# Layer 0 of a graph network: scores from x through one folded matrix, and h by rows only

## The chip, the cores and the metric

The kernel runs on one core of a Trainium2 chip. The metric is the device time of one execution in microseconds. A core has five engines that run side by side, each with its own queue of instructions: TensorE (PE in the profile; its weight loads are listed apart as PEld), VectorE (DVE), ScalarE (ACT), GpSimd (POOL) and SyncE (SP), which here issues loads. Within an engine the instructions go in the order in which they were built. Waits between engines go through semaphores.

## The reference

Four layers work on 16 batches of 1024 nodes with 128 features, `x`, and a 0/1 adjacency matrix `adj` of 1024 by 1024 per batch. Each layer adds its result to `x` and normalizes the rows. Only layer 0 is touched here:

```
h = x @ W_w.T + W_b
e = einsum('bjl,bkl->bjk', h @ A, h);  e = e + swapaxes(e, 1, 2)
att = where(adj > 0, e, -9e15);  att = softmax(att, axis=1) * adj
h_prime = relu(einsum('bij,bjk->bik', att, h))
coeff = sigmoid(concat([x, h_prime]) @ gate_w.T + gate_b)
x = layernorm(x + coeff * x + (1 - coeff) * h_prime)
```

Layer 1 thins out the adjacency row by row and then runs three steps of neighbour averaging; layer 2 is a second attention, and layer 3 a convolution on the graph.

Since e is summed with its transpose, e[j,k] = h_j (A + A') h_k. With h = W x + b this is x_j · (M x_k + v), where M = W'(A + A')W and v = W'(A + A')b, plus terms that hold no j. The softmax runs over j, so a term without j leaves it as it is.

## The kernel before

The work is written with pools of buffers and a framework that orders the instructions of each engine ahead of the run, by its own estimate of when each can start, and sets the semaphores. So the order on an engine isn't that of the source. The kernel has a fast path for the expected inputs, with checks collected in a flag, and a general kernel behind it that runs only where the flag is set.

In layer 0 three generators are interleaved by `in_turn`: `before` (batch b+1), `attention` (batch b) and `after` (batch b-1).

`before` goes through the eight blocks of 128 rows of the adjacency. For each, SP loads 512 KB into a ring of three buffers `an`; ScalarE turns it into 8-bit form (`carry` in the profile, L922) and sums the degree; VectorE checks the part right of the diagonal (L927); TensorE turns the finished blocks with narrow products (`pt`, L934), and VectorE compares them with the row block (`chk`, L935). Between these blocks the operands of the attention are made, all in float32: after block 1 the transpose `xT` of the rows `xn`; after block 3 `hT` = W0 xT + b0 and a part of the gate; after block 5 `G` = -As0 hT, with As0 = A + A'; after block 7 `hn`, which is `hT` turned back to rows. All of these, the `pt` products and the gates go through one pool of PSUM, `ps_h`, with two buffers of 512 columns.

`attention` takes eight blocks of 128 nodes k. ScalarE makes the mask (`msk`, L969); TensorE makes the negated scores of a block in two halves, with a block of `hT` as the stationary operand and `G` as the moving one (`pmm`, L724, in a pool `ps_w` of two buffers of 1024 columns); VectorE adds the mask and takes the minimum (`em`, `mx`, L972); ScalarE takes the exponential and its sum (L974); VectorE takes the reciprocal and scales a block of `hn` by it (`hs`, L976 and L978); TensorE accumulates `hs` times the exponentials into `acc` (L981). The two products of one block share the same `em` ring of two buffers.

`after` takes relu of `acc` as `hpT` (L987), makes the gate, turns `hpT`, mixes it with `xn` on VectorE (L998 to L1001) and normalizes the rows (`normed`): statistics on VectorE, a power on GpSimd (L745), a combined factor on VectorE (`ln_nb`, L799), and eight passes on ScalarE (L801).

A helper line stands for many operations in the profile: L724 is `wide_matmul`, L759 the turns, L766 the products over 512 columns, L775 the gates. `products` and `turned` yield a half of a result at a time, and the reading instruction follows in the source.

At the start the raw weights lie in a pool `l0_raw` that is closed before the pool `l0_work` is opened; the first buffer of `xn` lies where the raw weights lay. All loads of the layer go through SP's queue.

Of the kernel before, what the change touches and what calls it, by code (L numbers as in the profile page):

```python
# [9 lines left out]
F32 = mybir.dt.float32  # L10
# [5 lines left out]
FP8 = mybir.dt.float8e4  # L16
# [623 lines left out]
def fast_kernel(ctx: ExitStack, tc: tile.TileContext, t: dict, out: bass.AP, flag: bass.AP):  # L640
# [65 lines left out]
    def transposed(pool, psum, src, name, tag="tr"):  # L706
        v = pool.tile([P, P], F32, name=name)
        p = psum.tile([P, P], F32, name="wtr", tag=tag)
        nc.tensor.transpose(p, src, identf)
        nc.vector.tensor_copy(v, p)  # L710
        return v
# [178 lines left out]
    with ExitStack() as ph:  # L890

        early = ph.enter_context(tc.tile_pool(name="l0_early", bufs=1, reuse_waits="tile"))
        wts = ph.enter_context(tc.tile_pool(name="l0_w", bufs=1, reuse_waits="tile"))
        ps_w = ph.enter_context(tc.tile_pool(name="l0_pw", bufs=2, space=PSUM, reuse_waits="tile"))
        ps_a = ph.enter_context(tc.tile_pool(name="l0_pa", bufs=1, space=PSUM, reuse_waits="tile"))
        ps_h = ph.enter_context(tc.tile_pool(name="l0_ph", bufs=2, space=PSUM, reuse_waits="tile"))

        with tc.tile_pool(name="l0_raw", bufs=1) as raw:
            W0T = transposed(wts, ps_h, matrix(raw, t["L0_gnn_W_w"], "l0W"), "l0WT", "h")
            As0 = symmetric(wts, ps_h, matrix(raw, t["L0_gnn_A"], "l0A"), "l0As", "h")  # L900
        work = ph.enter_context(tc.tile_pool(name="l0_work", bufs=1, reuse_waits="tile"))
        small = ph.enter_context(tc.tile_pool(name="l0_small", bufs=2, reuse_waits="tile"))
        b0 = column(wts, t["L0_gnn_W_b"], "l0b")
        gw = wts.tile([P, 2, 32], F32, name="l0gw")
        nc.vector.memset(gw, 0.0)
        with nc.allow_non_contiguous_dma(reason="a vector of 256"):
            nc.sync.dma_start(gw[:, :, 0], t["L0_gnn_gate_w"].rearrange("o (h d) -> d (o h)", d=P))
        gb = row_bcast(wts, t["L0_gnn_gate_b"], 1, "l0gb")
        gbh = wts.tile([P, 1], F32, name="l0gbh")
        nc.vector.tensor_scalar(gbh, gb, 0.5, None, op0=OP.mult)  # L910
        nbig = wts.tile([P, 1], F32, name="l0nbig")
        nc.vector.memset(nbig, BIG)

        def before(s, b):

            s.xn = work.tile([P, NT, P], F32, name="xn", bufs=3)
            nc.sync.dma_start(s.xn, nat(t["x"][b]))
            for it in range(NT):
                c = b * NT + it
                an = early.tile([P, N], F32, name="an", bufs=3)  # L920
                nc.sync.dma_start(an, t["adj"][b][it * P:(it + 1) * P, :])
                nc.scalar.activation(Y[b][:, it, :], an, AF.Copy, accum_out=deg[:, c:c + 1], saturate=False)  # L922

                chk = early.tile([P, N], FP8, name="chk")
                done = (it + 1) * P
                if done < N:
                    nc.vector.scalar_tensor_tensor(chk[:, done:], an[:, done:], 0.0, an[:, done:], op0=OP.is_gt,  # L927
                                                   op1=OP.not_equal, accum_out=other[:, 3 * c:3 * c + 1], saturate=False)
                for h in range(it // 4 + 1):
                    js = range(4 * h, min(4 * h + 4, it + 1))  # L930
                    k = slice(js[0] * P, (js[-1] + 1) * P)
                    pt = ps_h.tile([P, 512], F32, name="pt", tag="h")
                    for i, jt in enumerate(js):
                        nc.tensor.matmul(pt[:, i * P:(i + 1) * P], Y[b][:, jt, it * P:done], identb, start=True, stop=True)  # L934
                    nc.vector.scalar_tensor_tensor(chk[:, k], pt[:, :k.stop - k.start], 0.0, an[:, k], op0=OP.is_gt,  # L935
                                                   op1=OP.not_equal, accum_out=other[:, 3 * c + h + 1:3 * c + h + 2],
                                                   saturate=False)
                if it == 1:
                    xT = early.tile([P, N], F32, name="xT")
                    for p, c, _ in turned(ps_h, s.xn):  # L940
                        nc.scalar.copy(xT[:, c], p)
                elif it == 3:
                    s.hT = work.tile([P, N], F32, name="hT", bufs=2)
                    for p, c in products(ps_h, (W0T, xT)):
                        nc.scalar.activation(s.hT[:, c], p, AF.Identity, bias=b0)
                    pz = gates(ps_h, early.tile([P, N], FP8, name="chk").bitcast(F32), (gw[:, 0, :], xT))
                    s.gx = small.tile([P, NT], F32, name="gx")
                    nc.vector.tensor_copy(s.gx.rearrange("p (q t) -> p q t", t=2), pz[:, :, :, 0])
                elif it == 5:
                    s.G = work.tile([P, N], F32, name="G", bufs=2)  # L950
                    for p, c in products(ps_h, (As0, s.hT)):
                        nc.scalar.activation(s.G[:, c], p, AF.Copy, scale=-1.0)
                elif it == 7:
                    s.hn = work.tile([P, N], F32, name="hn")
                    for p, c, _ in turned(ps_h, s.hT):
                        nc.vector.tensor_copy(s.hn[:, c], p)
                yield
            nc.gpsimd.dma_start(adj8_d[b], Y[b].bitcast(F32))

        def attention(s, b):  # L960


            s.acc = ps_a.tile([P, N], F32, name="acc")
            for jt in range(NT):
                js = slice(jt * P, (jt + 1) * P)
                c = b * NT + jt
                mn = mx0[:, c:c + 1]
                msk = work.tile([P, N], BF16, name="msk", bufs=2)
                nc.scalar.activation(msk, Y[b][:, jt, :], AF.Identity, scale=-BIG, bias=nbig)  # L969
                e = wide_matmul(ps_w, s.hT[:, js], s.G)  # L970
                em = work.tile([P, N], F32, name="em", bufs=2)
                nc.vector.tensor_tensor_reduce(em, e, msk, 1.0, 3.0e38, op0=OP.add, op1=OP.min, accum_out=mn)  # L972
                sm = small.tile([P, 1], F32, name="sm")
                nc.scalar.activation(em, em, AF.Exp, scale=-1.0, bias=mn, accum_out=sm)  # L974
                rs = small.tile([P, 1], F32, name="rs")
                nc.vector.reciprocal(rs, sm)  # L976
                hs = small.tile([P, P], F32, name="hs")
                nc.vector.tensor_scalar(hs, s.hn[:, js], rs, None, op0=OP.mult)  # L978
                for h in range(H2):
                    c = slice(h * 512, (h + 1) * 512)  # L980
                    nc.tensor.matmul(s.acc[:, c], hs, em[:, c], start=(jt == 0), stop=(jt == NT - 1))  # L981
                yield

        def after(s, b):

            hpT = work.tile([P, N], F32, name="hpT")
            nc.scalar.activation(hpT, s.acc, AF.Relu)  # L987
            pz = gates(ps_h, work.tile([P, NT, P], F32, name="r").rearrange("p t d -> p (t d)")[:, :N // 4], (gw[:, 1, :], hpT))
            co = small.tile([P, NT], F32, name="co")
            nc.vector.tensor_add(co.rearrange("p (q t) -> p q t", t=2), pz[:, :, :, 0],  # L990
                                 s.gx.rearrange("p (q t) -> p q t", t=2))
            nc.scalar.activation(co, co, AF.Tanh, scale=0.5, bias=gbh)
            cx = small.tile([P, NT], F32, name="cx")
            nc.vector.tensor_scalar(cx, co, 0.5, 1.5, op0=OP.mult, op1=OP.add)
            nc.vector.tensor_scalar(co, co, -0.5, 0.5, op0=OP.mult, op1=OP.add)
            yield
            r = work.tile([P, NT, P], F32, name="r")
            nc.vector.tensor_mul(s.xn, s.xn, per_row(cx))  # L998
            for p, c, k in turned(ps_h, hpT):
                nc.vector.tensor_mul(r[:, k, :], tiles3(p), half_rows(co[:, k]))  # L1000
            nc.vector.tensor_add(s.xn, s.xn, r)  # L1001
            yield
            normed(small, s.xn)
            nc.gpsimd.dma_start(nat(x1_d[b]), s.xn)
            yield

        in_turn(before, attention, after)
# [746 lines left out]
```

## Time and profile before

| What | Value |
|---|---|
| Median of 3 runs | 2961.86 us (2958.01 to 2962.2) |
| The profiled execution | 2964.0 us |
| Its span, first to last instruction | 2962.2 us |
| TensorE busy, share of the span | 2725.4 us, 92% |
| TensorE weight loads | 1695.2 us, 57% |
| VectorE busy | 2196.2 us, 74% |
| ScalarE busy | 2024.2 us, 68% |
| GpSimd busy | 325.8 us, 11% |
| First accumulation of layer 0 starts (L981) | 36.5 us |
| First and last relu of `acc` (L987) | 74.2 and 674.3 us |

Busy times overlap between engines. The ends of matmul records are modelled, so that two following records of TensorE overlap in the profile; the distance between their starts is what one costs in a row. A float32 product shows as two records. An "idle before" of an engine is put down to what released it last; where it says "issue", the profile shows nothing that it waited for. The median of the three runs and the profiled execution are different executions.

### The profile page before, as it was taken

Reading aid. Unit: us, or ns where it says so; the run is one execution under the profiler, and the core shown is the slowest. Engines: PE = TensorE matmul, PEld = TensorE weight load, DVE = VectorE, ACT = ScalarE, POOL = GpSimd, SP = SyncE. Lnnn points to the kernel's source line nnn. Section 1 sums busy time; section 2 is a strip of 40 time slices with the busy share of each in tenths; the row PEclk is TensorE's granted clock in tenths of the full one; section 3 lists DMA queues with packets and bytes.
Section 4 is the critical chain, followed back from the end, with each engine's and each line's share of the span. In section 5 each row is a group of like instructions: output and inputs, shape, how many; then the busy total and the mean of one; then the engine's idle time right before and its main releaser. Section 6 shows DMA issues by size and latency. Waiting matters only on the chain.

```text
span 2962.2 us, 42088 instructions
## 1 busy us (share of the span) xinstructions
PE 2725.4 (92%) x14771; PEld 1695.2 (57%) x14834; DVE 2196.2 (74%) x6087; ACT 2024.2 (68%) x3476; POOL 325.8 (11%) x295
## 2 busy tenths in 40 slices
PE   7999999996999889999899988999999999999996
PEld 3444444443666657877788873555555555555554
DVE  5777777777999976776688785777777777776765
ACT  6788888874788786666555435666666667676753
POOL 0000000030000001111122230001000101000000
PEclk9999999997999999999999997999999999999998
DMA  5444444420000052233467681111111111111000
GB/s 187 135 157 151 163 163 157 151 91 16 2 2 2 2 195 82 100 107 136 162 212 266 228 327 50 47 62 64 61 68 69 60 58 57 57 57 57 22 15 23
DMA packets 124125, 297.91 MB, mean 101 GB/s; under 512 B 12672, under 2 KB 65664, under 8 KB 116736
## 3 DMA queue, kind: packets, MB, share of 16 engines
q1 hardware_dynamic: 103440, 211.65, 21.6%
q0 software_dynamic: 20464, 83.47, 7.1%
q8 instruction: 119, 1.95, 0.3%
q14 instruction: 102, 0.84, 0.1%
HBM read 211.04 MB, written 84.02 MB: 100 GB/s over the span
## 4 chain that ended last, share of the span: by engine, by line
PE 36%; issue 19%; DVE 17%; POOL 4%; ACT 4%; DMA 2%; SPq 0%; POOLq 0%; DVEq 0%; ACTq 0%
PE ph L1550 8%; PE acc L1306 7%; PE ph L766 5%; PE acc L1626 4%; PE ph L1410 3%; PE pmm L724 3%; POOL ln_rstd L745 2%; PE ph L759 2%; DVE ln_st L794 2%; PE ph L1536 2%; DVE em L1612 2%; ACT xn L801 2%; POOL rn L745 1%; DVE A L1679 1%; PE acc L981 1%
## 5 line engine op out<-in xcount | busy, mean ns | idle before, releaser
L724 PE MATMUL pmm<-G,hT 128*128 128x512 f32 x1024 | 512.8, 614 | 10.7 <-DVE mx L1612 6.7
L801 ACT ACTIVATE xn<-xn,ln_nb,ln_rstd 128x128 f32<-128x128 f32 x512 | 207.4, 481 | 112.9 <-DVE ln_nb L799 112.8
L724 PEld LDWEIGHTS pmm<-G,hT 128*128 128x128 f32 x1024 | 175.0, 193 | 166.7 <-issue 118.3
L745 POOL TENSOR_TENSOR ln_rstd<-ln_rstd,mhalf 128x8 f32<-128x8 f32 (+1 forms) x68 | 115.9, 1704 | 1323.9 <-DVE nmx L1614 606.7
L1306 PE MATMUL acc<-a,lo 128*128 128x512 f32 x768 | 243.5, 401 | 15.5 <-DVE lo L1273 15.5
L1626 PE MATMUL acc<-em,hs 128*128 128x512 f32 x512 | 251.8, 611 | 3.5 <-DVE hs L1623 1.9
L981 PE MATMUL acc<-em,hs 128*128 128x512 f32 x512 | 245.7, 601 | 6.5 <-DVE hs L978 5.6
L1306 PE MATMUL acc<-a,hi 128*128 128x512 f32 x768 | 244.1, 402 | 3.7 <-ACT hi L1272 3.5
L1145 ACT ACTIVATE q<-s,negc 128x512 f16<-128x512 f32 x256 | 170.6, 697 | 59.2 <-DVE negc L1124 22.3
L1143 PE MATMUL s<-step,carry 128*128 128x384 bf16 (+3 forms) x1034 | 199.4, 304 | 7.9 <-DVE carry L1113 3.2
L1157 ACT ACTIVATE carry<-pc,negone 128x512 fp8e4<-128x512 f32 x256 | 166.8, 699 | 38.3 <-PE pc L1156 28.9
L972 DVE CUSTOM_DVE_ANT_0 em<-pmm,msk 128x1024 f32<-128x1024 f32 x128 | 155.9, 1218 | 40.6 <-PE acc L981 20.3
L1306 PEld LDWEIGHTS acc<-a,lo 128*128 128x128 f32 x768 | 144.4, 190 | 54.8 <-DVE lo L1273 21.1
L1612 DVE CUSTOM_DVE_ANT_0 em<-pmm,msk 128x1024 f32<-128x1024 f32 x128 | 155.6, 1216 | 25.9 <-PE acc L1626 21.3
L922 ACT ACTIVATE carry<-an 128x1024 fp8e4<-128x1024 f32 x128 | 134.4, 1050 | 50.7 <-DMA an<-in_adj 50.5
L1306 PEld LDWEIGHTS acc<-a,hi 128*128 128x128 f32 x768 | 143.0, 190 | 37.1 <-ACT hi L1272 4.0
L1607 ACT ACTIVATE msk<-A,nbig 128x1024 bf16<-128x1024 fp8e4 x128 | 145.9, 1140 | 26.6 <-DVE mx L1612 23.4
L974 ACT ACTIVATE em<-em,mx 128x1024 f32<-128x1024 f32 x128 | 146.0, 1141 | 25.4 <-DVE mx L972 22.7
L981 PEld LDWEIGHTS acc<-em,hs 128*128 128x128 f32 x512 | 90.9, 189 | 123.9 <-issue 87.2
L1410 PE MATMUL ph<-Wx,hT 128*128 128x128 f32 x768 | 153.4, 282 | 3.0 <-ACT nT L1435 1.4
L1410 PE MATMUL ph<-Wr,ag 128*128 128x128 f32 x768 | 151.1, 279 | 1.4 <-DMA ag<-ag_d 1.2
L1666 ACT CAST A<-A 128x1024 fp32r<-128x1024 fp8e4 x64 | 64.2, 1040 | 124.8 <-PE ph L1550 124.6
(294 smaller groups left out, 6181.9 us busy)
## 6 DMA issues: line engine op xcount, KB each, us to landing
an<-in_adj SPq DMA_DIRECT2D x128, 512.0 KB, 3.5
adj_d<-carry POOLq DMA_DIRECT2D x16, 1024.0 KB, 4.2
A<-dil_d SPq DMA_DIRECT2D x16, 1024.0 KB, 7.1
rdeg<-rdeg_d SPq DMA_DIRECT2D x32, 512.0 KB, 4.2
ag_d<-ag POOLq DMA_DIRECT2D x32, 512.0 KB, 5.3
ag<-ag_d SPq DMA_DIRECT2D x32, 512.0 KB, 6.3
A<-adj_d SPq DMA_DIRECT2D x16, 1024.0 KB, 4.7
xn<-in_x SPq DMA_DIRECT2D x16, 512.0 KB, 4.2
```

What stands on the lines that cost most here:

```text
L724: nc.tensor.matmul(p[:, h * 512:(h + 1) * 512], lhsT, rhs[:, h * 512:(h + 1) * 512], start=True, stop=True)
L745: nc.gpsimd.tensor_tensor(r, r, mhalf[:, :n], op=OP.pow)
L801: nc.scalar.activation(r[:, k.start + i, :], r[:, k.start + i, :], AF.Identity, scale=rstd[:, i:i + 1], bias=nb[:, i:i + 1])
L981: nc.tensor.matmul(s.acc[:, c], hs, em[:, c], start=(jt == 0), stop=(jt == NT - 1))
L1143: nc.tensor.matmul(s[:, lo or 0:], y, twos if lo is None else step[:, :512 - lo], start=(j == 0), stop=(j == len(terms) - 1))
L1145: nc.scalar.activation(q[:, h * 512:(h + 1) * 512], s, AF.Abs, bias=st.negc[:, i:i + 1])
L1157: nc.scalar.activation(Y[b][:, hb, ks], pc, AF.Relu, bias=negone, saturate=False)
L1306: nc.tensor.matmul(acc, part[:, jt, :], pieces[h * NT // 2 + i][:, j, :], start=(jt == 0 and p == 0), stop=(jt == NT - 1 and p == 1))
L1410: nc.tensor.matmul(p[:, i * P:(i + 1) * P], x[:, j * P:(j + 1) * P], W, start=(n == 0), stop=(n == 1))
L1550: nc.tensor.matmul(p, part[:, jt, :], A[:, jt, c], start=(jt == 0 and i == 0), stop=(jt == NT - 1 and i == 1))
L1612: nc.vector.tensor_tensor_reduce(em, e, msk, 1.0, 0.0, op0=OP.add, op1=OP.max, accum_out=mx)
L1626: nc.tensor.matmul(s.acc[:, c], hs, em[:, c], start=(jt == 0), stop=(jt == NT - 1))
```

## The change

Ahead of the batches two more matrices and a vector are computed: AW = As0 W0, M0 = W0' AW and nu = -AW' b0. `G` is made from `xT` directly, as -(M0 xT) + nu, after block 3, where `hT` was made. `hT` is gone: the scores take a block of `G` as the stationary operand and `xT` as the moving one. `xT` moves to the pool `l0_work` with two buffers. `hn` is made by eight products of a block of `xT` with W0T, after block 6, and VectorE adds the bias, which is loaded as a row to all partitions. As0 moves to the raw pool, and the raw pool also holds AW and the bias as a column.

```diff
         with tc.tile_pool(name="l0_raw", bufs=1) as raw:
-            W0T = transposed(wts, ps_h, matrix(raw, t["L0_gnn_W_w"], "l0W"), "l0WT", "h")
-            As0 = symmetric(wts, ps_h, matrix(raw, t["L0_gnn_A"], "l0A"), "l0As", "h")
+            W0 = matrix(raw, t["L0_gnn_W_w"], "l0W")
+            W0T = transposed(wts, ps_h, W0, "l0WT", "h")
+            As0 = symmetric(raw, ps_h, matrix(raw, t["L0_gnn_A"], "l0A"), "l0As", "h")
+            AW = raw.tile([P, P], F32, name="l0AW")
+            p = ps_h.tile([P, P], F32, name="wtr", tag="h")
+            nc.tensor.matmul(p, As0, W0, start=True, stop=True)
+            nc.vector.tensor_copy(AW, p)
+            M0 = wts.tile([P, P], F32, name="l0M")
+            p = ps_h.tile([P, P], F32, name="wtr", tag="h")
+            nc.tensor.matmul(p, W0, AW, start=True, stop=True)
+            nc.vector.tensor_copy(M0, p)
+            nu = wts.tile([P, 1], F32, name="l0nu")
+            p = ps_h.tile([P, 1], F32, name="wtr", tag="h")
+            nc.tensor.matmul(p, AW, column(raw, t["L0_gnn_W_b"], "l0b"), start=True, stop=True)
+            nc.vector.tensor_scalar(nu, p, -1.0, None, op0=OP.mult)
...
-        b0 = column(wts, t["L0_gnn_W_b"], "l0b")
+        b0 = row_bcast(wts, t["L0_gnn_W_b"], P, "l0brow")
...
                 if it == 1:
-                    xT = early.tile([P, N], F32, name="xT")
+                    s.xT = work.tile([P, N], F32, name="xT", bufs=2)
                     for p, c, _ in turned(ps_h, s.xn):
-                        nc.scalar.copy(xT[:, c], p)
+                        nc.scalar.copy(s.xT[:, c], p)
                 elif it == 3:
-                    s.hT = work.tile([P, N], F32, name="hT", bufs=2)
-                    for p, c in products(ps_h, (W0T, xT)):
-                        nc.scalar.activation(s.hT[:, c], p, AF.Identity, bias=b0)
-                    pz = gates(ps_h, early.tile([P, N], FP8, name="chk").bitcast(F32), (gw[:, 0, :], xT))
+                    s.G = work.tile([P, N], F32, name="G", bufs=2)
+                    for p, c in products(ps_h, (M0, s.xT)):
+                        nc.scalar.activation(s.G[:, c], p, AF.Identity, scale=-1.0, bias=nu)
+                    pz = gates(ps_h, early.tile([P, N], FP8, name="chk").bitcast(F32), (gw[:, 0, :], s.xT))
...
-                elif it == 5:
-                    s.G = work.tile([P, N], F32, name="G", bufs=2)
-                    for p, c in products(ps_h, (As0, s.hT)):
-                        nc.scalar.activation(s.G[:, c], p, AF.Copy, scale=-1.0)
-                elif it == 7:
+                elif it == 6:
                     s.hn = work.tile([P, N], F32, name="hn")
-                    for p, c, _ in turned(ps_h, s.hT):
-                        nc.vector.tensor_copy(s.hn[:, c], p)
+                    for p, c, blocks in halves(ps_h):
+                        for i, k in enumerate(blocks):
+                            nc.tensor.matmul(p[:, i * P:(i + 1) * P], s.xT[:, k * P:(k + 1) * P], W0T, start=True, stop=True)
+                        nc.vector.tensor_add(tiles3(s.hn[:, c]), tiles3(p), b0[:, None, :].to_broadcast([P, 4, P]))
...
-                e = wide_matmul(ps_w, s.hT[:, js], s.G)
+                e = wide_matmul(ps_w, s.G[:, js], s.xT)
```

## The prediction

> **What bounds the kernel now.** I read the page's slices first (layer 0 is about the first nine of 40), then stretches of 40 us, then TensorE in order of time, since the change stays in layer 0. A stretch from its middle; columns are length, then busy time of TensorE, weight load, VectorE, ScalarE, GpSimd, then clock and DMA:
>
> ```profile
> 300.00:340.00 40.00, 39.77 (x155) 18.38 (x154) 30.29 (x100) 34.96 (x61) 3.81 (x4) 1.00 0.50 163
> ```
>
> TensorE shows 39.8 us of 40, ScalarE 35.0, VectorE 30.3. But its ends are modelled, so I count from start to start. Three parts of TensorE's timeline (start, length, engine, line, operation, count, wait before it) give the prices:
>
> ```profile
> 310.78 1.88 PE L766 MATMUL ph<-hT,l0As 128*128 128x512 f32 x4
> 312.50 1.88 PE L981 MATMUL acc<-em,hs 128*128 128x512 f32 x4
> ...
> 324.25 1.04 PE L759 MATMUL ph<-identf,hpT 128*128 128x128 f32 x8
> 325.12 2.74 PE L724 MATMUL pmm<-G,hT 128*128 128x512 f32 x6
> ...
> 1501.34 0.38 PE L1410 MATMUL ph<-Wx,hT 128*128 128x128 f32 x2
> 1501.56 0.39 PE L1410 MATMUL ph<-Wr,ag 128*128 128x128 f32 x2
> ```
>
> The first pair: a float32 product of 512 columns is two records of 0.43 us, so the two halves (x4) take 1.72 us. The second: eight transposes take 0.87, or 0.109 each. The third, from layer 1: a float32 product with 128 columns and a new stationary operand each time takes 0.22 (1501.34 to 1501.56), two records.
>
> The starts of the L775 gates on hpT mark the batches: 280.6, 320.7, 359.9, 401.9 and so on: 40.1, 39.2, 42.0, then 39.7, 39.2, 42.0. The period is 40.3 us, in three alternating orders. TensorE's work per batch: 32 halves of the two attention products 27.5 (32 x 0.86), the two 512-column products on each of W0T and As0 3.44, three sets of turns 2.62, 36 narrow `pt` products 2.0 (0.056 each), gates 1.14 (16 records of 0.071), their four turns 0.44: 37.2. So 3.1 us per batch are gaps: small ones of about 0.05 at some 40 changes of operand, and real waits such as these:
>
> ```profile
> 413.15 1.08 PE L724 MATMUL pmm<-G,hT 128*128 128x512 f32 x2
> 415.01 1.55 PE L981 MATMUL acc<-em,hs 128*128 128x512 f32 x3 [0.78 <-DVE hs L978]
> ...
> 372.12 1.98 PE L724 MATMUL pmm<-G,hT 128*128 128x512 f32 x4
> 375.13 1.12 PE L766 MATMUL ph<-xT,l0WT 128*128 128x512 f32 x2 [1.03 <-DVE chk L935]
> ```
>
> The second is a product waiting for one of only two `ps_h` buffers, which the symmetry check on VectorE still holds. TensorE's waits from 100 to 640 us, summed:
>
> ```profile
> PE ph L766 <- DVE chk L935: 5.2, 5, 1.0
> PE acc L981 <- DVE hs L978: 3.7, 6, 0.8
> PE pt L934 <- ACT xT L941: 2.5, 5, 0.5
> PE pmm L724 <- DVE mx L972: 1.6, 4, 0.4
> ```
>
> So layer 0 is set by TensorE's own work, with a small part of VectorE's lateness.
>
> **What the Trainium skill says.** "FP8 and Floating Point Precision", section "TensorE Precision Notes": true float32 takes four passes. The trace agrees: four passes of a 128-column product should be about twice 0.109, and it measures 0.22. "Perfetto Trace Analysis", section "Transposes", asks for transposes rather than products, since they skip arithmetic; here a turn costs half of the product that replaces it. The same page, "Identifying the Most-Contended Engine", warns that matmul busy time is a poor measure; the 39.8 of 40 hides the 3 us of gaps counted above.
>
> **Per batch, part by part.** Removed: the As0 product, 1.72 us of TensorE, and eight turns of hT, 0.87. Added: eight products of xT blocks with W0T, 8 x 0.222 = 1.78. The W0T product becomes the M0 product at the same size, and the attention product keeps its form with operands exchanged. Net on TensorE: 36.4 instead of 37.2, or -0.81 us.
>
> ScalarE loses a pass over two halves. Before, hT cost 2 x 0.67 and G 2 x 0.59; now G with a bias costs 2 x 0.67. That is -1.18 us, worth nothing by itself while TensorE is behind. VectorE's two copies of 0.68 (L956) become additions with a broadcast row. Copy and addition from PSUM cost the same here (L956: 683 ns; L1412, the same form of addition: 684), so nothing. Two buffers fewer pass through the crowded `ps_h` pool.
>
> **The gaps.** The built order on every engine tells what follows. Instead of three orders in turn there is one, the same for eleven batches, with 37 groups on TensorE per batch where there were 38 to 42. I walked it once round by hand with the starts of the old trace (check of 512 columns 0.62, mask and maximum 1.13, exponential 1.13, LayerNorm statistics 2.2, the GpSimd power 1.7 to 1.85). Three waits stand out. The second half of xn's turn waits about 0.75 for the check of 256 columns, which now stands behind the mask operation and an addition of 1.2 on VectorE (the orders of before that I read have it behind one or the other, not both). The M0 product and the attention half beside it wait 0.3 each. Against that, the check of 384 columns now always stands ahead of the VectorE instruction that waits 1.4 to 1.6 for GpSimd; the order with 42.0 has it behind, and the 1.03 above is its price. The new `hn` additions stand ahead of two checks, but the last attention product of the batch covers them (1.72 against 1.2). The walk ends at 2.6 of gaps; I take 2.7, since it skips some small ones. Period 36.4 + 2.7 = 39.1, so -1.2 us per batch, and 15 batches run so beside an attention: -18 us.
>
> **The start.** The xn load at 10.15 takes the memory of the raw weights, so it waits for the last use of them, now As0's addition:
>
> ```profile
> 10.15 0.38 SPq L917 DMA_DIRECT2D xn<-in_x  x1
> 9.85 0.28 DVE L839 TENSOR_TENSOR l0As<-l0A,wtr 128x128 f32<-128x128 f32 x1
> ```
>
> In the new order the raw pool holds AW and the bias too, and xn waits for three more products in a chain (some 0.5 to 0.6 each in the slow start, by the 0.42 to 0.47 of the first turns) and two copies of 0.28 between them, with semaphores some 2.5 us; one more load on SP ahead of the adjacency tiles adds 0.5. Behind xn on SP stand all later adjacency tiles, and the check on VectorE stands behind the copies: +3 us for all that follows. Given back: G comes straight from xT, without the As0 product, which ran from 25.15 to 28.45, and hn one step earlier. By the same prices the first accumulation, at 36.51 now, starts near 34.5. Net -2, between -5 and +3.
>
> After layer 0 the order of all five engines is the same as before, so the shift is carried to the end unchanged.
>
> Sum: the profiled execution took 2964.0 (span 2962.2 and 1.8 around it); -18 - 2 gives 2944. The median of the runs shown is 2.1 below the profiled one, so 2942 for it.
>
> **Rivals.** (1) Larger gain: the single order is as tight as the best of the old three, whose gaps I count at 1.6. Then 36.4 + 1.6 = 38.0, -2.3 x 15 - 2 = -36: 2926. For it: ScalarE is freed too. Against: the xn wait in the walk. (2) Hidden: the loop through LayerNorm, GpSimd and the checks on VectorE sets the period, and TensorE's saving becomes wait. Only the start counts: 2957 to 2965, taken as 2960. For it: these waits are in the trace at that place. Against: VectorE is idle 10 us of each 40. (3) Slower: the check of 256 columns, late behind the mask operation and the addition, holds both turns of xn, hence xT, and every product after it, and the one order repeats this in every batch. Its price is up to the 1.2 of the addition plus the 1.13 of the mask operation, 2.3 a batch; it decides from gaps of 3.9 (3.1 plus the 0.81 saved). At 4.7 gaps: +0.8 x 15 = +12, 2974. For it: `ps_h` has two buffers, and this is the pool that TensorE waits on now. Against: VectorE catches up within the batch. (4) It doesn't do what it says: a guard sends the run to the general kernel. Only `mn`, compared with 1e15, changes, and by terms constant along the softmax. I give it no chance worth a number.
>
> **How the numbers follow.** Chances: main case 0.50, (1) 0.18, (2) 0.17, (3) 0.15. What can be told from no change is 0.2%, 5.9 us. Main case and (1) are faster nearly always; (2) is split between faster and same. So faster 0.75, same 0.11, slower 0.14. The range: the unknown sizes are the gaps (1.6 to 3.9 and above), times 15, and the start (-5 to +3). From 2927, near rival (1), to 2966, which takes in (2) and the near half of same; about 0.05 lies below, 0.15 above. The main case alone: 2934 to 2952.
>
> **What would show it.** Right: gates on hpT at a steady 39 apart; no L766 rows on As0; the first xn load near 13 and the first accumulation at 34 to 35; layer 0's last accumulation near 652 instead of 672. Wrong: a gap of over 1 us before the second xn turn in each batch, ended by the check; periods of 40 or more; a start of accumulation after 38; or any shift after layer 0.

## The result, and the profile after

The changed kernel takes 2944.83 us (median of six runs, 2943.01 to 2946.11); the kernel before took 2959.69 beside it (six runs, 2954.01 to 2962.2). The ratio is 0.9949, 95% interval 0.9937 to 0.9961: faster by half a per cent. In the groups of runs further down the kernel before stood at 2960.0 to 2960.6. The profiled execution took 2946.11 with a span of 2944.3, so 17.9 less than the profiled one before; that is 3.0 more than the medians differ, since the profiled execution before lay 4.3 above its median and this one 1.3.

All line numbers are now those of the changed kernel: L935 is the conversion to 8-bit form, L940 and L948 the checks, L954 the copies to `xT`, L966 the products for `hn` and L967 their bias addition, L980 the mask, L983 the minimum, L985 the exponential, L992 the accumulation, L998 the relu of `acc`. First the stretch that was shown for the kernel before (length, then busy time of TensorE, weight load, VectorE, ScalarE, GpSimd, then clock, DMA share and GB/s):

```profile
300.00:340.00 40.00, 39.29 (x160) 18.36 (x158) 31.10 (x104) 34.25 (x59) 3.17 (x3) 1.00 0.49 162
```

It looks as before: TensorE 39.3 of 40 against 39.8. A stretch as full as this can't show a change of 2%, so the batches are measured from start to start. In TensorE's timeline the gates on `hpT` started at 75.28, then up to 643.59 (the 15th) and 675.38 (the 16th) before; now at 74.50, 627.96 and 658.20. The 14 distances average 40.59 before and 39.53 after: -1.06 per batch. That makes -14.9 over 14 batches; the first gate adds -0.8, the last distance (31.79 to 30.24) -1.5: -17.2 where layer 0 ends. From the last gate to the end the profiled executions take 2286.8 and 2286.1, so nothing is won or lost behind it.

TensorE's waits from 100 to 640 us, summed (what waited, what released it, us in total, times, longest):

```profile
PE pq L775 <- ACT hpT L998: 10.9, 13, 1.8
PE pmm L724 <- DVE mx L983: 1.1, 1, 1.1
PE ph L766 <- DVE chk L948: 1.0, 1, 1.0
PE pt L947 <- ACT xT L954: 0.5, 1, 0.5
PE ph L759 <- ACT xT L954: 0.4, 1, 0.4
```

The four waits that the view showed before, 13.0 in all, are nearly gone. In their place stands one that I had not foreseen: the gates wait for the relu of `acc`, 0.84 on average in 13 batches. All waits together are 13.9, so by waits of this size nothing was won. Its place in TensorE's timeline (start, length, engine, line, operation, count, wait before it):

```profile
424.46 1.95 PE L966 MATMUL ph<-l0WT,xT 128*128 128x128 f32 x16
426.25 1.88 PE L992 MATMUL acc<-em,hs 128*128 128x512 f32 x4
427.96 0.61 PE L947 MATMUL pt<-identb,carry 128*128 128x128 bf16 x8
428.41 1.94 PE L724 MATMUL pmm<-xT,G 128*128 128x512 f32 x4
431.67 0.64 PE L775 MATMUL pq<-hpT,l0gw 128*32 128x256 f32 x8 [1.32 <-ACT hpT L998]
```

The eight products for `hn` take 424.46 to 426.25, 1.79 us or 0.224 each: the predicted price. The last accumulation of the batch ends near 428, and the gates start at 431.67. In between ScalarE does this (its timeline, from 425):

```profile
425.44 1.13 ACT L980 ACTIVATE msk<-carry,l0nbig 128x1024 bf16<-128x1024 fp8e4 x1
429.56 1.06 ACT L935 ACTIVATE carry<-an 128x1024 fp8e4<-128x1024 f32 x1 [2.98 <-DMA an<-in_adj]
430.52 0.19 ACT L935 ACTIVATION_READ_ACCUMULATOR carry<-an 128x1 f32 x1
430.61 1.00 ACT L998 ACTIVATE hpT<-acc 128x1024 f32<-128x1024 f32 x1
```

The relu could have run from 428 on. It stands behind the conversion of an adjacency block, and that waits 2.98 us for its load. The Trainium skill, "Perfetto Trace Analysis", section "Tensor Engine Instruction (MATMUL, LD_WEIGHTS)", says that ScalarE and VectorE execute strictly in order; this is that rule with a price on it. The load could be issued only when VectorE had finished its check of block 6, since the ring has three buffers and this is the second block of the next batch. The last reader of the buffer on VectorE:

```profile
424.20 0.55 DVE L948 SCALAR_TENSOR_TENSOR chk<-pt,an 128x384 fp8e4<-128x384 f32 x1
424.68 0.08 DVE L948 DVE_READ_ACCUMULATOR chk<-pt,an 128x1 bf16 x1
```

and the load behind it on SP:

```profile
424.82 0.33 SPq L934 DMA_DIRECT2D an<-in_adj  x1
```

Issued at 424.82, usable at 429.56: 4.7 us. ScalarE's waits for adjacency loads grew from 37.6 to 57.5 between 100 and 640 us.

The other batches confirm the chain. In 12 batches in a row this load is issued 2.71 us before TensorE starts the last record of the accumulation, and the wait of the gates is the load's time less 3.4 us: a load that takes 5.17 gives a wait of 1.78, one of 3.75 a wait of 0.36. What is new is the order on ScalarE. Before the change the last conversion ahead of the relu was that of block 0 in 13 of 14 batches, and from 190 to 600 us it never waited for its load. Now it is that of block 1, in all 14.

### The profile page after: what moved, and what is told of

It reads as the page before. It is cut to its first block, busy times and chain, and to the rows that moved or that the text cites. A ratio compares the mean times of both kernels' runs of the same rounds, so it can differ in the third digit from the quotient of the medians.

```text
span 2944.3 us, 42230 instructions
## 1 busy us (share of the span) xinstructions
PE 2706.1 (92%) x14841; PEld 1691.9 (57%) x14904; DVE 2197.1 (75%) x6090; ACT 2007.6 (68%) x3444; POOL 325.1 (11%) x295
## 4 chain that ended last, share of the span: by engine, by line
PE 41%; DVE 21%; issue 21%; ACT 6%; POOL 5%; DMA 5%; SPq 0%; POOLq 0%; DVEq 0%; ACTq 0%
PE ph L1561 8%; PE acc L1317 6%; PE ph L766 5%; PE pmm L724 5%; PE acc L992 4%; PE acc L1637 4%; POOL ln_rstd L745 3%; DVE ln_st L794 3%; PE ph L1421 2%; DMA an<-in_adj 2%; PE ph L759 2%; PE ph L1547 2%; DVE em L1623 2%; ACT xn L801 2%; POOL rn L745 1%
## 5 line engine op out<-in xcount | busy, mean ns | idle before, releaser
L724 PE MATMUL pmm<-xT,G 128*128 128x512 f32 x512 | 257.5, 611 | 2.6 <-DVE mx L983 1.1
L724 PE MATMUL pmm<-G,hT 128*128 128x512 f32 x512 | 250.3, 610 | 7.2 <-DVE mx L1623 6.5
L992 PE MATMUL acc<-em,hs 128*128 128x512 f32 x512 | 246.1, 603 | 2.5 <-DVE hs L989 0.5
L1168 ACT ACTIVATE carry<-pc,negone 128x512 fp8e4<-128x512 f32 x256 | 166.5, 698 | 37.5 <-PE pc L1167 27.5
L983 DVE CUSTOM_DVE_ANT_0 em<-pmm,msk 128x1024 f32<-128x1024 f32 x128 | 156.3, 1221 | 41.6 <-PE pmm L724 23.5
L935 ACT ACTIVATE carry<-an 128x1024 fp8e4<-128x1024 f32 x128 | 134.5, 1051 | 70.5 <-DMA an<-in_adj 70.0
L985 ACT ACTIVATE em<-em,mx 128x1024 f32<-128x1024 f32 x128 | 146.1, 1141 | 17.3 <-DVE mx L983 13.5
L992 PEld LDWEIGHTS acc<-em,hs 128*128 128x128 f32 x512 | 87.2, 190 | 105.9 <-issue 62.6
```

The source lines that it names most:

```text
L724: nc.tensor.matmul(p[:, h * 512:(h + 1) * 512], lhsT, rhs[:, h * 512:(h + 1) * 512], start=True, stop=True)
L1168: nc.scalar.activation(Y[b][:, hb, ks], pc, AF.Relu, bias=negone, saturate=False)
```

## The experiments

All runs stand in one table. "Distance" is the mean of the 14 distances between the first 15 gates on `hpT` (12 for e2_twice, whose orders alternate in threes), from one profiled execution of each kernel; "work" is TensorE's work per batch counted as in the prediction; "gaps" is the difference. "Check behind" counts, from 120 to 640 us, how often the check of 384 columns of block 2 stands on VectorE directly behind `ln_nb`, the LayerNorm factor that waits for GpSimd.

| run | median us | ratio to before, 95% | first gate | distance | work | gaps | check behind |
|---|---|---|---|---|---|---|---|
| before | 2959.7 | | 75.3 | 40.59 | 37.2 | 3.4 | 5 of 13 |
| changed | 2944.8 | 0.9937 to 0.9961 | 74.5 | 39.53 | 36.4 | 3.2 | 1 of 13 |
| e1_an4 | 2935.2 | 0.9894 to 0.9924 | 72.7 | 39.06 | 36.4 | 2.7 | 0 of 13 |
| e5_start | 2946.9 | 0.9932 to 0.9965 | 68.4 | 39.87 | 36.4 | 3.5 | 0 of 13 |
| e6_both | 2941.6 | 0.9914 to 0.9950 | 68.5 | 39.09 | 36.4 | 2.7 | 0 of 12 |
| e8_hpT_dve | 2966.5 | 1.0010 to 1.0027 | 74.2 | 40.71 | 36.4 | 4.3 | 13 of 13 |
| e2_twice | 2972.7 | 1.0026 to 1.0059 | 69.4 | 41.71 | 38.1 | 3.6 | 4 of 13 |
| e2b_rows_twice | 3002.3 | 1.0121 to 1.0165 | 77.9 | 43.18 | 38.1 | 5.0 | 12 of 12 |
| e3_scores | 2955.4 | 0.9973 to 0.9990 | 73.2 | 40.29 | 37.2 | 3.1 | 6 of 13 |
| e4_rows | 2994.4 | 1.0099 to 1.0144 | 75.5 | 42.82 | 38.1 | 4.7 | 12 of 12 |
| e4b_rows6 | 2970.4 | 1.0017 to 1.0046 | 72.3 | 41.14 | 38.1 | 3.0 | 6 of 13 |
| e9_hn7 | 2950.9 | 0.9956 to 0.9982 | 75.8 | 39.86 | 36.4 | 3.5 | 0 of 13 |
| e10_an4_hn7 | 2947.8 | 0.9947 to 0.9977 | 72.0 | 39.70 | 36.4 | 3.3 | 0 of 13 |
| e12_hn5 | 2971.7 | 1.0023 to 1.0045 | 76.0 | 41.03 | 36.4 | 4.7 | 12 of 13 |

One sum holds for the whole table. Count TensorE's work between the same gates, by the prediction's prices, and take off the waits over 0.15 us that the profile shows there. Of each distance 2.0 to 2.5 us are then left in all 14 kernels, while these waits range from 0.5 to 2.8. So the distance is work, plus the waits, plus a nearly fixed rest. From the kernel before to the changed one the waits go from 1.16 to 1.09 and the rest from 2.39 to 2.28.

My theory was that TensorE's work sets the time and that the saved 0.81 us per batch is the gain. The rivals were that the freer order made it, or that TensorE's work is hidden behind a loop of loads, ScalarE and VectorE.

The edits are shown against the changed kernel where nothing else is said. **The new wait: a fourth adjacency buffer.** The statistics of LayerNorm get one buffer less to make room; no run made that part of the edit alone.

```
-                an = early.tile([P, N], F32, name="an", bufs=3)
+                an = early.tile([P, N], F32, name="an", bufs=4)
...
-            st = small.tile([P, NT, 6], F32, name="ln_st")
+            st = small.tile([P, NT, 6], F32, name="ln_st", bufs=stats)
...
-            normed(small, s.xn)
+            normed(small, s.xn, stats=1)
```

> The changed kernel with four buffers for the adjacency blocks instead of three (and one buffer fewer for the LayerNorm statistics, to make room). Theory A (ring): the second block of the next batch is loaded only when the check of block 6 has freed a buffer, ScalarE waits for it with the relu of acc queued behind, and TensorE waits 10.9 us in 13 batches at the gates on hpT. With a fourth buffer that wait falls below 2 us in all, and the time to about 2934 (-0.8 x 14 from 2945). Rival B (TensorE would find another late partner at once, VectorE): the wait moves, time 2942 to 2947.

2935.15, so another 9.7 below the changed kernel, and faster than both by more than the intervals. In the steady batches TensorE's order is the one of the changed kernel, ScalarE's is not. TensorE's waits:

```profile
PE pq L775 <- ACT hpT L998: 5.5, 12, 1.1
PE pmm L724 <- DVE mx L983: 0.5, 1, 0.5
PE acc L992 <- DVE hs L989: 0.2, 1, 0.2
```

The wait for `hpT` is halved, from 10.9 to 5.5; I had it under 2. ScalarE still waits for loads ahead of the relu, for a shorter time:

```profile
420.87 1.06 ACT L935 ACTIVATE carry<-an 128x1024 fp8e4<-128x1024 f32 x1 [2.12 <-DMA an<-in_adj]
421.83 0.19 ACT L935 ACTIVATION_READ_ACCUMULATOR carry<-an 128x1 f32 x1
421.92 1.00 ACT L998 ACTIVATE hpT<-acc 128x1024 f32<-128x1024 f32 x1
```

The buffer did not do what I expected. From the third batch on, the framework put one conversion more ahead of the relu, that of block 2 where the changed kernel has block 1. So the relu stands behind a load that is just as late: it is again issued 2.71 us before the last record of the accumulation starts. The wait is shorter because this load takes less time, 3.84 on average over 12 batches instead of 4.24; why it does is not shown.

So this run confirms the chain from the load over the conversion and the relu to TensorE. It does not show that a longer ring brings the load forward. "Perfetto Trace Analysis", section "Optimization Strategy", says that a gap that repeats on the engine that should be full can mean too few buffers for the next tile. This case agrees in part only: the edit brought 9.7 us, or 0.33%, and 5.4 of them are this gap by the profile, but the gap stayed in nearly every batch, because the built order used the buffer up.

**The start: raw weights that don't lie under `xn`.**

```
-        with tc.tile_pool(name="l0_raw", bufs=1) as raw:
+        raw = wts
+        if True:
```

> The changed kernel with the raw weights kept in the weights' pool, so that the first load of xn shares no memory with them. If the start lies on the path (the theory of the prediction: the chain of three small products holds xn and all loads behind it by 3 us), the first accumulation comes about 3 us earlier than 37.5 and the time falls by 3, to 2942. If the start is set by the order on VectorE and ScalarE instead, the first accumulation moves by less than 1 us and the time stays at 2944 to 2946.

2946.85, no difference from the changed kernel. The first accumulation came at 33.74 instead of 37.54 and the first gate 6.1 earlier. But the distances grew from 39.53 to 39.87, and the last gate was only 1.3 earlier. TensorE's waits show where the head start went (L999 is the same relu, one line further down):

```profile
PE pq L775 <- ACT hpT L999: 15.8, 13, 2.0
```

The wait for `hpT` rose from 10.9 to 15.8. Time won at the start is lost again to the same wait. In the three batches that I compared, TensorE, VectorE and ScalarE have the order of the changed kernel, and the load is again issued 2.71 us before the last record of the accumulation. But it takes 4.58 on average over 12 batches instead of 4.24, and the wait grows by as much. What slows the load there stays open.

**Both together.** Four buffers as above, and a first tile in the work pool so that `xn` doesn't lie where the raw weights lay:

```
         work = ph.enter_context(tc.tile_pool(name="l0_work", bufs=1, reuse_waits="tile"))
+        work.tile([P, N], F32, name="hpT")
```

> Both: four adjacency buffers, and the first xn on other memory than the raw weights. If the two waits are independent, the gains add: about 2931 under theory A with the start on the path; 2934 if the start is worth nothing; 2945 if neither is on the path.

2941.55, between the two, where the sum was expected. In layer 0 it is what was expected: the first gate at 68.49, distances of 39.09, the last gate at 645.96, 12.2 before that of the changed kernel. Against the run with four buffers alone the first gate is 4.2 earlier and the last one still 3.8, so here a head start was kept. But from there to the end its profiled execution takes 2296.8, against 2286.1. Part of that may be TensorE's clock, granted at 0.93 from 1300 to 1400 us, against 0.98 in the run with four buffers alone. Its six runs spread over 12 us, 2934.76 to 2947.18; the rest of the loss behind layer 0 stays open.

**The relu on VectorE.**

```
-            nc.scalar.activation(hpT, s.acc, AF.Relu)
+            nc.vector.tensor_scalar(hpT, s.acc, 0.0, None, op0=OP.max)
```

> The changed kernel with the relu of acc on VectorE instead of ScalarE, the ring left at three. Theory A: the late load still holds ScalarE, but hpT is no longer behind it, so TensorE's 0.84 us per batch at the gates go, less what 1.1 us more of VectorE per batch costs: 2934 to 2942. Rival C (acc itself is late, not ScalarE's queue): the wait at the gates stays near 0.8 per batch and the time is 2945 or more.

2966.49, slower than the kernel before: the expectation fell. The wait for `hpT` is gone, but TensorE's waits are now these:

```profile
PE ph L766 <- DVE chk L948: 13.4, 13, 1.0
PE pmm L724 <- DVE mx L983: 13.2, 13, 1.1
PE ph L759 <- ACT xT L954: 3.7, 9, 1.8
```

The first is the wait that the kernel before had in one order of three, now in every batch. Moving one instruction to another engine gave the whole layer another built order. VectorE also has the relu to do in each batch, so this run can't tell the relu's cost there from that of the order, which comes back below.

**More work of the same kind.** First the product of M0 twice, in place:

```
                     for p, c in products(ps_h, (M0, s.xT)):
+                        nc.tensor.matmul(p, M0, s.xT[:, c], start=True, stop=True)
```

> The changed kernel with the product of M0 and xT issued twice into the same place (the second overwrites the first with the same values): TensorE gets 1.72 us more per batch. Theory (TensorE's own work sets the period, the gaps stay): +1.72 x 16 = +27, so near 2972. Rival (the loop through loads, ScalarE and VectorE sets the period, TensorE's work fills its waits): 0 to +8, so below 2953. In between, the share says how much of TensorE's work counts.

2972.72: 27.9 above the changed kernel, as if all of the 1.72 x 16 = 27.5 counted. The agreement is in part luck. The gaps grew by about 0.5 per batch in three alternating orders, and a first gate 5 us earlier gave that back. But that TensorE's work is hidden is excluded.

Then the products for `hn` twice:

```
                             nc.tensor.matmul(p[:, i * P:(i + 1) * P], s.xT[:, k * P:(k + 1) * P], W0T, start=True, stop=True)
+                            nc.tensor.matmul(p[:, i * P:(i + 1) * P], s.xT[:, k * P:(k + 1) * P], W0T, start=True, stop=True)
```

> The changed kernel with each of the eight products for hn issued twice: +1.78 us of TensorE per batch, just ahead of the place where the gates wait 0.84 per batch for hpT. If TensorE's work counts in full: +28, so near 2973. If the wait for hpT hangs on a load alone (the ring of three adjacency buffers), it shrinks by as much as the work grows and takes 0.84 of the 1.78: +15, so near 2960. If TensorE is not the bound there: below 2950.

3002.33, so +57.5, and none of the three expectations holds. The distance grew by 3.65: 1.78 of work and 1.9 of new gaps. The check of 384 columns now stands behind `ln_nb` in all 12 batches.

**One part of the change at a time.** The scores part keeps hT by columns for `hn` alone (the lines for `hn` after block 6 are taken out, and b0 is loaded as a column):

```
+                elif it == 5:
+                    s.hT = work.tile([P, N], F32, name="hT")
+                    for p, c in products(ps_h, (W0T, s.xT)):
+                        nc.scalar.activation(s.hT[:, c], p, AF.Identity, bias=b0)
+                elif it == 7:
...
+                    for p, c, _ in turned(ps_h, s.hT):
+                        nc.vector.tensor_copy(s.hn[:, c], p)
```

> The scores part of the change alone: G from xT through M0, but hT is still made by columns (after block 5, where the product of As0 was) and turned to hn after block 7. This leaves the eight products out and puts a product of W0T and eight turns in: TensorE's work per batch is 37.2 again, as before the change. Theory of work: near 2960, same as before. Rival (the change gained by freeing the order, since G no longer hangs on hT): near 2945, like the changed kernel.

2955.39: work as before, gaps of 3.1 instead of 3.4, so 0.3 x 15 = 4.5 from the order alone, and 4.6 measured. So the rival gets about a third of the gain, not all of it.

The rows part keeps hT, As0 and the scores of before, and makes `hn` from `xT`, after block 7 as before, with one buffer for the statistics. The main lines of its edit, against the kernel before:

```
-                    for p, c, _ in turned(ps_h, s.hT):
-                        nc.vector.tensor_copy(s.hn[:, c], p)
+                    for p, c, blocks in halves(ps_h):
+                        for i, k in enumerate(blocks):
+                            nc.tensor.matmul(p[:, i * P:(i + 1) * P], s.xT[:, k * P:(k + 1) * P], W0T, start=True, stop=True)
+                        nc.vector.tensor_add(tiles3(s.hn[:, c]), tiles3(p), brow[:, None, :].to_broadcast([P, 4, P]))
```

> The other part of the change alone: scores from hT and As0 as before, hT stays by columns, but hn comes by eight products of xT with W0T and a bias row after block 7, instead of eight turns of hT. TensorE's work per batch is 37.2 + 1.78 - 0.87 = 38.1. Theory of work: +0.91 x 15 = +14, near 2974, and slower than before. Rival (gaps shrink with the one order, or the work is hidden): 2962 or less.

2994.42, 20 more than the work explains. The gaps are 4.7, and again the check stands behind `ln_nb` in every batch.

**The order with the work unchanged.** Three runs move the products for `hn` by a block; one of them has the fourth adjacency buffer as well. After block 7 instead of 6, with three and with four adjacency buffers:

```
-                elif it == 6:
+                elif it == 7:
```

> The changed kernel with the products for hn after block 7 instead of block 6. Same work on every engine. In the built order seven of these products and an attention half (2.4 us) now stand on TensorE between the last accumulation and the gates on hpT, and three attention halves (2.6 us) between the narrow pt products and the first M0 half, where the changed kernel has four. If the wait for hpT is what is left to gain: -0.8 x 14, so near 2934. If the wait only moves to another place: 2943 or more.

> As the run before it, with four adjacency buffers. If the ring mattered only through the wait for hpT, which the place of hn has then already taken away: equal to the run before it, near 2934. If the ring also holds up other things: near 2928.

2950.85 and 2947.76. No gain over the changed kernel in either. For the first run the rival was right, that the wait only moves; both numbers expected of the second, 2934 and 2928, were missed. TensorE's waits in the first:

```profile
PE pmm L724 <- DVE mx L983: 6.1, 13, 0.5
PE acc L992 <- DVE hs L989: 2.6, 13, 0.2
PE acc L992 <- ACT G L958: 2.0, 3, 1.0
```

The wait for `hpT` (10.9) is gone, since ScalarE has block 0 as the last conversion ahead of the relu again, in 13 of 14 batches; 10.7 stand elsewhere. The fourth buffer, worth 9.7 with `hn` after block 6, gives 3.1 here, within the spread of the runs. That fits a value that hung mostly on the wait for `hpT`.

After block 5:

```
-                elif it == 6:
+                elif it == 5:
```

> The changed kernel with the products for hn after block 5 instead of block 6. Same work on every engine, but the built order has only two attention halves (1.7 us) between the pt products of block 4 and the first M0 half, where the changed kernel has four (3.4 us). Theory that this distance sets a wait of about 1.0 per batch for the check on VectorE, as in the two slow experiments with the products for hn: +1.0 to +1.8 per batch, so 2960 to 2971. Theory of work alone: 2945.

2971.65: the same work, 26.8 slower than the changed kernel and slower than the kernel before. The largest of its waits, 12.4 us in 12 batches where the changed kernel has 1.0, shows in VectorE's timeline of that run:

```profile
413.62 0.82 DVE L940 SCALAR_TENSOR_TENSOR chk<-an 128x640 fp8e4<-128x640 f32 x1
...
416.00 0.17 DVE L799 SCALAR_TENSOR_TENSOR ln_nb<-ln_mv,ln_rstd 128x8 f32<-128x8 f32 x1 [1.55 <-POOL ln_rstd L745]
416.08 0.55 DVE L948 SCALAR_TENSOR_TENSOR chk<-pt,an 128x384 fp8e4<-128x384 f32 x1
```

and in TensorE's:

```profile
413.46 0.38 PE L947 MATMUL pt<-identb,carry 128*128 128x128 bf16 x4 [0.51 <-ACT xT L954]
413.68 1.98 PE L724 MATMUL pmm<-xT,G 128*128 128x512 f32 x4
416.70 1.13 PE L766 MATMUL ph<-xT,l0M 128*128 128x512 f32 x2 [1.03 <-DVE chk L948]
```

The `pt` products are done before 414. Their check could have run at 414.4, but it stands behind `ln_nb`, which waits 1.55 for GpSimd's power. The buffer comes free near 416.6, and the M0 product starts at 416.70. That is over half of what TensorE waits longer in this run, 34.6 in all against 13.9; the rest are waits for `hs` (6.4) and, ahead of the `pt` products, for the copies to `xT` (5.6). In the changed kernel VectorE has the two the other way round:

```profile
404.72 0.56 DVE L948 SCALAR_TENSOR_TENSOR chk<-pt,an 128x384 fp8e4<-128x384 f32 x1
405.20 0.09 DVE L948 DVE_READ_ACCUMULATOR chk<-pt,an 128x1 bf16 x1
406.47 0.17 DVE L799 SCALAR_TENSOR_TENSOR ln_nb<-ln_mv,ln_rstd 128x8 f32<-128x8 f32 x1 [1.18 <-POOL ln_rstd L745]
```

Last, the rows part with `hn` after block 6 (against e4_rows):

```
-                elif it == 7:
+                elif it == 6:
```

> The rows part alone, with the products for hn after block 6 instead of block 7. Same work as the other run of the rows part (2994), TensorE 38.1 per batch. The built order alternates: one batch with three attention halves between the pt products and the W0T product, one with two (the other run: two in every batch). Theory of the distance: every second batch loses the wait of 1.0 and what follows from it, so -0.5 to -0.8 per batch on average, 2982 to 2987. If that distance doesn't matter: 2994. If only the work counted: 2974.

2970.4, against 2994 for the same work one block later, and better than the theory of the distance had it. With gaps of 3.0 the rows part costs 10.4 over the kernel before. By the table that is +0.91 x 15 = 13.7 of work and 0.4 x 15 = 6.0 less in gaps, so about 8.

The table says one thing more. Where the check stands behind `ln_nb` in nearly every batch the gaps are 4.3 to 5.0; where in none, or one, 2.7 to 3.5; where in every second or third batch, 3.0 to 3.6.

The scores part shows it best, since its two orders alternate and give TensorE the same work between the gates: distances of 41.1 to 41.5 with the check behind, 39.2 without. Of the 2 us between them the profile shows 1.03 at the M0 product and 0.51 at the `pt` products behind it.

In e4b_rows6 the distances are 43.2 and 38.7 in turn, but they can't be compared as they stand. The order puts 18 halves of the scores between the gates of one batch and 14 in the next. With 0.86 for a half that is 41.5 and 40.4 for 16 halves, so the batch with the wait takes 1.1 longer. The wait costs in each batch where it comes, and coming in every second one it costs half as much on average. No run moved that one check alone.

## Why the prediction was right, and where not

**Time and sign.** 2942 was predicted and 2944.83 measured; the sum for the profiled execution was 2944 and it took 2946.11. The range and the main case's own range hold it. As a gain, about 20 was predicted; the medians give 14.9 and the profiled executions 17.9, and the kernel before had itself come out 2.2 faster than the median the prediction started from.

**TensorE's work: right.** 0.81 per batch from four prices; the one new price, the `hn` product, measured 0.224 for 0.222. (The prediction set four passes against twice a turn; the narrow bf16 `pt` products of the same shape are the plainer measure: eight take 427.96 to 428.41, 0.056 each, and the float32 product takes four times that.) That this work counts is shown by the doubled M0 product (+27.9) and by the rows part in a good order (+10.4). 15 batches make 12 of the 17.9 us.

**The gaps: right in direction, smaller, and not by the waits of the walk.** The walk gave 2.7 from 3.1. Counted in one way in both kernels they are 3.2 from 3.4, so -0.25 per batch instead of -0.4. That they shrank at all was luck: the waits lost at one place came back at another, 13.0 before and 13.9 after. Three things in the step:

The wait of 0.75 of the second turn of `xn` behind the check of 256 columns did not come. In the changed kernel that turn starts on TensorE at

```profile
401.01 0.64 PE L759 MATMUL ph<-identf,xn 128*128 128x128 f32 x4
```

while VectorE's check begins only at

```profile
401.23 0.42 DVE L948 SCALAR_TENSOR_TENSOR chk<-pt,an 128x256 fp8e4<-128x256 f32 x1
```

and ScalarE has just emptied the first half of the turn:

```profile
400.36 0.59 ACT L954 COPY xT<-ph 128x512 f32<-128x512 f32 x1 [0.54 <-PE ph L759]
```

So the second half took the buffer that the copy freed at 400.95, not the one that the check held. The walk let the two buffers of `ps_h` alternate, and they don't have to.

The wait for `hpT`, 0.84 per batch, was missing: I walked round TensorE and VectorE, and left ScalarE out because it had become freer. It has less work, but the new order puts the conversion of block 1 ahead of the relu, and that one waits for a load. The run with `hn` after block 7 has block 0 there again, and no such wait.

The step on the check of 384 columns, which "now always stands ahead" of the instruction that waits for GpSimd, was right in 12 of 13 batches, and by the experiments more weighty than I had it: with the check behind in as many, the same work takes 2971.65. The 42.0 of that order is not its price alone, though: 17 halves of the scores lie between those gates, against 16 in the batch of 39.2.

**The start: wrong.** I had -2 with a first accumulation at 34.5; it came at 37.54, later than before, and the first gate gained 0.8. The cost was right: `xn` was loaded at 13.43, where 13 was predicted. Part of the return came too: the first scores started at 26.46 instead of 28.87. What failed is "`hn` one step earlier". VectorE's timeline of the changed kernel:

```profile
36.32 0.16 DVE L987 RECIPROCAL rs<-sm 128x1 f32<-128x1 f32 x1 [1.50 <-ACT em L985]
36.40 0.67 DVE L967 TENSOR_TENSOR hn<-ph,l0brow 128x512 f32<-128x512 f32 x1
37.10 0.29 DVE L989 TENSOR_SCALAR hs<-hn,rs 128x128 f32<-128x128 f32 x1
```

The products for `hn` started at 34.53, but their addition stood behind the reciprocal of block 1, which waited for its exponential, which stood on ScalarE behind a conversion that waited for a load. It is the same pattern as the wait for `hpT`. With three adjacency buffers the size matters little: the run with the early start gained 6.1 at the first gate, and its median was no better. With four, most of a head start lasted to the end of the layer.

**After layer 0: right,** 2286.8 and 2286.1. The layer's last accumulation starts at 656.5 where it started at 673.7; 652 had been named.

**The rivals.** The first took 1.6 for the gaps of the tightest old order; from the 39.2 shown it is 39.2 - 37.2 = 2.0, so it stood nearer to 38.4 per batch than to 38.0. This larger gain did not come by itself, but the run with a fourth buffer comes half the way to it (2935). "Hidden" is excluded by the doubled product. The slower one was a real danger: its price, 2974 at gaps of 4.7, is what e12_hn5 shows with 2971.65 at 4.7, though at the check of 384 columns and not at that of 256.

## What to carry to other kernels

Where TensorE is nearly full, as here, a change of its work counts, but what the framework makes of the order can weigh more: 12 us of work were saved, and moving `hn` by one block cost 26.8. So the built order of every engine has to be read, not only that of the engine with the work. Look on each in-order engine for an instruction that waits for something slow (a load, GpSimd) with one behind it that TensorE needs. And after an edit that should end such a wait, read the order again: here the framework used the fourth adjacency buffer to put another conversion ahead of the relu, which then stood behind a load just as late.

Compare batches only with the work between the marks counted: orders that alternate move work across the mark, 3.4 us of it in e4b_rows6.

## What was not expected

A load issued at the same point of TensorE's work in every batch, 2.71 us before one accumulation record, took 3.7 to 5.4 us in the changed kernel and in the one with the early start, and TensorE waited for all of it beyond 3.4. With that, a head start of 6 us was eaten within a layer that TensorE fills to nine tenths, though the order and the work of the engines were the same.
